# Layer norms in a four-layer transformer stack: the reciprocal root on GpSimd instead of ScalarE and VectorE

## The chip, the cores and the metric

The kernel runs on one core of a Trainium2 chip. A core has five engines with instruction queues of their own, each worked through in order: TensorE (PE in the profile; PEld is its weight load), VectorE (DVE), ScalarE (ACT), GpSimd (POOL) and SyncE (SP, which issues DMAs). The metric is the time of one execution on the device in microseconds (us); shown are three runs and one profiled execution.

## The reference

The input x has 4 x 256 tokens of 256 features, float32. Four layers follow each other, each with an attention to a small context and a feed-forward part, both gated and added to x:

```python
x = x + tanh(g_xattn[i]) * xattn_i(layernorm(x), ctx)
x = x + tanh(g_ffn[i]) * ffn_i(layernorm(x))

def _layernorm(x, axis=-1, eps=1e-05):
    m = jnp.mean(x, axis=axis, keepdims=True)
    v = jnp.var(x, axis=axis, keepdims=True)
    return (x - m) / jnp.sqrt(v + eps)
```

The layers differ. Layer 0: 16-head attention through a latent with rotary positions, and 16 experts of which 6 are used per token, beside a shared one. Layer 1: latent attention, and a feed-forward part with ternary weights and GELU. Layer 2: 16-head attention with a causal mask, and a single matrix with weights and tokens quantised to 8 bits. Layer 3: such attention, and 8 experts of which 2 are used, with a shared one. The output is x, 1024 x 256.

## The kernel before, in words

x stays in SBUF for the whole kernel, as 8 tiles of 128 tokens x 256 features. The tiles are worked on in two groups of four (512 tokens, `TPG` = 4 tiles to a group).

`layernorm(g, scalar, after)`, L425 to L453, normalises one group. VectorE computes the statistics of each tile (bn_stats L430, bn_aggr L433) into `mv`, 128 x 4 x 2. ScalarE takes the root of variance + eps for the four tiles at once, 128 x 4 (L435), and VectorE its reciprocal (L438), so that `rstd` holds a number for every token. Then each tile is shifted and scaled into `xn`: by VectorE in one instruction (L449), or, with `scalar=True`, by ScalarE (L446) from a `shift` that VectorE prepares (L442). `transposed` (L455 to L464) has PE transpose the four tiles (L461) into two PSUM buffers and copies them into `xT`; `evacuate` (L165 to L171) gives such copies by turns to ScalarE (L169) and to VectorE (L171). The projections (L476 and others) read `xT`.

The function is called 16 times, for two groups in each of the 8 half layers: in `attention0` (L722 for the first group and L805 for the second), `normalised` (L465, for the experts of layers 0 and 3), `attention1` (L950), `inputs1` (L1874, the feed-forward part of layer 1), at the end of that part for layer 2's first group (L1940), in the queries of layers 2 and 3 (L1045), and in `rounded` (L1998, the quantised part of layer 2). `rounded` and layer 3's queries pass `scalar=True`. At L805 two hints of order are passed as `after`: the first tile's statistics and the root are placed behind named instructions (`behind`, L141), without a semaphore.

ScalarE evaluates functions from tables that are loaded when the set changes (ACT_TABLE_LOAD rows). At the start a dummy activation on a 128 x 1 tile (`root`, L189 and L190) loads a table. The other functions are the exponential of the softmax (L484, and L1101 in layers 2 and 3), Tanh (L822, once), Silu (L1677, L1789 and in the experts) and Gelu (L1912).

Attention runs through `in_flight` (L519): for step i the scores and exponentials of token tile i are begun, `weights` (L486) normalises tile i-1 (VectorE sums L490 and reciprocal L491, then GpSimd multiplies 128 x 1024, L492), tile i-2 is transposed by PE (L506), copied by ScalarE (L507) and multiplied with the values (L714 in layers 0 and 1; L1109 and L1121 in layers 2 and 3), and tile i-3 is added to x (L517). The norms of the next half layer begin as soon as their four tiles of x are done, so the first group's norm often runs while the last tiles of attention are in flight.

GpSimd also does half of the rotary arithmetic, memsets, the indirect DMAs of the experts (L1386, L1485) and, in layer 2's quantised part, the additions to x (L2013, L2035). `ffn2` ends with matmuls that have no result (`kept_busy`, L510 to L514) while PE would otherwise have none.

The order of each engine's queue is made by the framework's scheduler from the data dependencies, priorities and hints such as those named; the kernel doesn't write it out. Tiles from pools (`xn`, `rstd`, `mv`) come round in a ring of buffers.

Of the kernel before, what the change touches and what calls it, by code (L numbers as in the profile page):

```python
# [30 lines left out]
F32 = mybir.dt.float32  # L31
# [4 lines left out]
AF = mybir.ActivationFunctionType  # L36
ALU = mybir.AluOpType
AX = mybir.AxisListType

P = 128  # L40
# [5 lines left out]
TPG = TH // P  # L46
# [4 lines left out]
EPS = 1e-5  # L51
# [46 lines left out]
def tile_flamingo(ctx: ExitStack, tc: tile.TileContext, a: dict, out: bass.AP):  # L98
    nc = tc.nc

    const = ctx.enter_context(tc.tile_pool(name="const", bufs=1))
# [36 lines left out]
    def small(shape, name, bufs=3, dtype=F32):  # L138
        return sb.tile(shape, dtype, tag=name, name=name, bufs=bufs)

    def behind(later, sooner):  # L141

        tc.add_manual_dep(
            later.ins,
            sooner.ins.name,
            mybir.DependencyInfo(mybir.DependencyClass.NoSync, mybir.DependencyReason.DATA),
            reason="not sooner",
        )
# [37 lines left out]
    nc.gpsimd.memset(ones, 1.0)  # L186
    eps = const.tile([P, 1], F32, tag="eps", name="eps")
    nc.gpsimd.memset(eps, EPS)
    root = small([P, 1], "root", 1)  # L189
    nc.scalar.activation(root, eps, AF.Sqrt)  # L190


    fixed = const.tile([P, FIXED], F32, tag="fixed", name="fixed")
# [231 lines left out]
    def layernorm(g, scalar=False, after=()):  # L425

        mv = small([P, TPG, 2], "mv")
        for i in range(TPG):
            st = small([P, 6], "st")
            made = nc.vector.bn_stats(st, x[g * TPG + i])  # L430
            if after:
                behind(made, after[0])
            nc.vector.bn_aggr(mv[:, i, :], st)  # L433
        rstd = small([P, TPG], "rstd")
        made = nc.scalar.activation(rstd, mv[:, :, 1], AF.Sqrt, bias=eps)  # L435
        if after:
            behind(made, after[1])
        nc.vector.reciprocal(rstd, rstd)  # L438
        xn = []
        if scalar:  # L440
            shift = small([P, TPG], "shift")
            nc.vector.scalar_tensor_tensor(shift, mv[:, :, 0], -1.0, rstd, ALU.mult, ALU.mult)  # L442
        for i in range(TPG):
            n = sb.tile([P, D], F32, tag="xn", name="xn", bufs=AHEAD + 2)
            if scalar:
                nc.scalar.activation(n, x[g * TPG + i], AF.Identity, bias=shift[:, i : i + 1], scale=rstd[:, i : i + 1])  # L446
                xn.append(n)
                continue
            kept["normal"] = nc.vector.tensor_scalar(  # L449
                n, x[g * TPG + i], mv[:, i, 0:1], rstd[:, i : i + 1], ALU.subtract, ALU.mult  # L450
            )
            xn.append(n)
        return xn  # L453
# [11 lines left out]
    def normalised():  # L465

        out = []
        for g in range(NG):
            xn = layernorm(g)
            out.append((transposed(xn), xn))  # L470
        return out
# [247 lines left out]
    def attention0(gate):  # L719


        xT = [transposed(layernorm(0))]  # L722
        fold_queries0(0)
        after = kept["copied"], kept["folded"]
# [77 lines left out]
        for n in range(6 * NQ + 2):  # L802
            f, m = divmod(n, 6)
            if n == 2:
                xT.append(transposed(layernorm(1, after=after)))  # L805
            if f < NQ:
                rotated(n)
                if m == 1 and f + 1 < NQ:
                    fold_queries0(f + 1)
                if m % 3 == 1 and f >= NQ - 2:  # L810
                    next(output)
            if wide is None:
                wide, rest = fold_scores0()
            if m == 3 and f < NQ:
                to_latent(f, 0)
            if m == 5:
                rest_to_latent(f)
            if m == 1 and f >= 1:
                to_latent(f - 1, 1)
            if n >= 6:  # L820
                next(later, None)
# [1374 lines left out]
```

## Time and profile before

| | |
|---|---|
| three runs | 826.5, 824.56, 826.2 us; median 826.2 |
| profiled execution | 824.72 us, of which 822.9 the span of the trace |
| mean granted clock of TensorE | 0.992 |
| busy PE / PEld | 776.0 us (94%) / 520.6 us (63%) |
| busy DVE / ACT / POOL | 497.2 us (60%) / 291.7 us (35%) / 246.0 us (30%) |
| ACT_TABLE_LOAD | 21, of 1.283 us each |
| roots (L435) | 16, 0.298 us each |
| reciprocals of them (L438) | 16, 0.170 us each |

The profile is that of one execution. A group line names the source line, engine and operation, then output<-inputs, shapes and the number of instructions; after the first bar stand busy us and the mean ns of one, after the second the idle time of the engine just before them and the instruction that ended most of it. A line of the timeline gives the start and length in us of a run of like instructions, and in square brackets the idle time of the engine ahead of it with what released it. A line of waits gives the waiting instruction, the one it waited for, and the us in total, the times and the longest. The granted clock is TensorE's, as a share of full speed.

### The profile page before, as it was taken

Reading aid. Unit: us, or ns where it says so; the run is one execution under the profiler, and the core shown is the slowest. Engines: PE = TensorE matmul, PEld = TensorE weight load, DVE = VectorE, ACT = ScalarE, POOL = GpSimd, SP = SyncE. Lnnn points to the kernel's source line nnn. Section 1 sums busy time; section 2 is a strip of 40 time slices with the busy share of each in tenths; the row PEclk is TensorE's granted clock in tenths of the full one; section 3 lists DMA queues with packets and bytes.
Section 4 is the critical chain, followed back from the end, with each engine's and each line's share of the span. In section 5 each row is a group of like instructions: output and inputs, shape, how many; then the busy total and the mean of one; then the engine's idle time right before and its main releaser. Section 6 shows DMA issues by size and latency. Waiting matters only on the chain. (4 is left out here: it accounts for less than half of the span.)

```text
span 822.9 us, 12507 instructions
## 1 busy us (share of the span) xinstructions
PE 776.0 (94%) x4507; PEld 520.6 (63%) x4510; DVE 497.2 (60%) x1146; ACT 291.7 (35%) x508; POOL 246.0 (30%) x211
## 2 busy tenths in 40 slices
PE   6999999898999999999999999998798899999994
PEld 5544433787564776766556566755445647999993
DVE  5565455874693455534878759888769564334331
ACT  3121112343421333422543568166455421233320
POOL 1355444322123344222021110024424103444332
PEclk9999999999999999999999999999999999999998
DMA  9510115800121253333930001630000102232211
GB/s 358 181 39 0 58 39 190 281 18 11 30 63 50 68 130 73 64 74 81 336 111 1 8 1 33 229 129 1 26 1 2 52 9 78 54 50 42 29 16 18
DMA packets 32467, 62.44 MB, mean 76 GB/s; under 512 B 5552, under 2 KB 19504, under 8 KB 31696
## 3 DMA queue, kind: packets, MB, share of 16 engines
q1 hardware_dynamic: 25008, 51.91, 18.3%
q0 software_dynamic: 7104, 9.41, 6.9%
q8 instruction: 39, 0.64, 0.3%
q10 hardware_dynamic: 288, 0.26, 0.1%
q14 instruction: 28, 0.23, 0.1%
HBM read 52.81 MB, written 9.27 MB: 75 GB/s over the span
## 5 line engine op out<-in xcount | busy, mean ns | idle before, releaser
L492 POOL TENSOR_TENSOR attn<-attn,sm 128x1024 f32<-128x1024 f32 x32 | 61.1, 1911 | 219.3 <-DVE sm L491 170.9
L476 PE MATMUL wide<-xT,big 128*128 128x512 f32 (+1 forms) x240 | 108.6, 600 | 1.1 <-DVE shared L1678 0.9
L742 DVE TENSOR_TENSOR rope<-wide,big 128x512 f32<-128x512 f32 x96 | 59.6, 684 | 51.9 <-PE wide L476 51.9
L476 PEld LDWEIGHTS wide<-xT,big 128*128 128x128 f32 (+1 forms) x240 | 43.4, 188 | 57.3 <-issue 49.3
L1451 PE MATMUL wide<-blk,still 128*128 128x128 f32 x640 | 74.8, 275 | 0.6 <-DVE blk L1423 0.6
L1451 PEld LDWEIGHTS wide<-blk,still 128*128 128x128 f32 x640 | 73.1, 192 | 0.8 <-issue 0.8
L714 PE MATMUL mm<-vo,attnT 128*128 128x256 f32 x256 | 58.6, 382 | 1.5 <-ACT attnT L507 1.5
L476 PE MATMUL wide<-xT,dense 128*128 128x512 f32 (+1 forms) x120 | 55.1, 598 | 0.0
L714 PEld LDWEIGHTS mm<-vo,attnT 128*128 128x128 f32 x256 | 47.8, 190 | 11.4 <-ACT attnT L507 3.3
L507 ACT COPY attnT<-mm 128x512 f32<-128x512 f32 x64 | 34.5, 587 | 43.3 <-PE mm L506 42.9
L490 DVE TENSOR_REDUCE sm<-attn 128x16 f32<-128x1024 f32 x32 | 38.7, 1209 | 15.2 <-ACT attn L484 13.8
L1413 DVE COPY still<-big 128x1024 f32 x20 | 13.9, 694 | 52.1 <-PE wide L1451 44.5
L1485 POOL DMA_INDIRECT out_dram<-ring,scratch x20 | 31.5, 1577 | 39.5 <-DVE ring L1478 15.6
L1485 POOL DMA_INDIRECT sums<-ring,big x17 | 26.8, 1575 | 48.5 <-ACT ring L1567 18.9
L1469 PE MATMUL mm<-big,hidden 128*128 x160 | 37.8, 380 | 1.4 <-DVE hidden L1462 1.4
L506 PE MATMUL mm<-ident,attn 128*128 128x128 f32 x256 | 34.6, 279 | 4.6 <-POOL attn L492 4.6
L1386 POOL DMA_INDIRECT xs<-xd,scratch x20 | 20.0, 1002 | 62.1 <-PE mm L1420 31.5
L506 PEld LDWEIGHTS mm<-ident,attn 128*128 128x128 f32 x256 | 29.9, 143 | 12.8 <-POOL attn L492 7.9
L1461 ACT ACTIVATE hidden<-wide 128x512 f32<-128x512 f32 x20 | 12.0, 598 | 71.2 <-PE wide L1451 65.7
L476 PEld LDWEIGHTS wide<-xT,dense 128*128 128x128 f32 (+1 forms) x120 | 21.5, 185 | 24.4 <-issue 22.7
L517 DVE SCALAR_TENSOR_TENSOR x<-mm,tg,x 128x256 f32<-128x256 f32 x44 | 20.4, 469 | 26.6 <-PE mm L714 15.0
L796 ACT COPY big<-mm 128x512 f32<-128x512 f32 x16 | 8.6, 589 | 67.9 <-PE mm L784 61.7
(363 smaller groups left out, 1575.8 us busy)
## 6 DMA issues: line engine op xcount, KB each, us to landing
big<-in_L_w_gate_up SPq DMA_DIRECT2D x8, 1024.0 KB, 12.0
big<-in_L_w_down SPq DMA_DIRECT2D x8, 512.0 KB, 9.0
w_L_qk<-in_L_qk SPq DMA_DIRECT2D x4, 896.0 KB, 7.3
big<-in_L_w SPq DMA_DIRECT2D x2, 1480.0 KB, 8.1
big<-in_L_w SPq DMA_DIRECT2D x2, 1110.0 KB
big<-in_L_wo SPq DMA_DIRECT2D x1, 2048.0 KB, 15.3
big<-in_L_w SPq DMA_DIRECT2D x2, 1024.0 KB, 5.3
xd<-xn SPq DMA_DIRECT2D x16, 128.0 KB, 1.9
```

Source lines behind the costliest of these rows:

```text
L476: nc.tensor.matmul(ps, w(c), xT[:, c, :], start=(c == 0), stop=(c == 1))
L490: nc.vector.tensor_reduce(sm, e, AX.X, ALU.add)
L492: nc.gpsimd.tensor_tensor(e, e, sm.unsqueeze(2).to_broadcast([P, groups, n]), ALU.mult)
L506: nc.tensor.transpose(ps[:, i * P : (i + 1) * P], ev[:, pr * P : (pr + 1) * P], ident)
L507: nc.scalar.copy(aT[:, half * 4 : half * 4 + 4, :].rearrange("p i t -> p (i t)"), ps)
L517: return nc.vector.scalar_tensor_tensor(x[t], ps, gate, x[t], ALU.mult, ALU.add)
L714: nc.tensor.matmul(ps[:, :D], aT[:, s, :], vo[:, s, :], start=(s == 0), stop=(s == NP - 1))
L742: nc.vector.tensor_tensor(m[:, s, :].rearrange("q (b t) -> q b t", t=S), ps[:, s, :].rearrange("q (b t) -> q b t", t=S), table, ALU.mult,)
L1386: nc.gpsimd.indirect_dma_start(out=xs, out_offset=None, in_=self.xd, in_offset=bass.IndirectOffsetOnAxis(ap=self.gather[:, b : b + 1].bitc ...
L1451: made = nc.tensor.matmul(ps[:, k, f : f + P], w[:, at : at + P], st[:, c * P : (c + 1) * P], start=(c == 0), stop=(c == 1),)
L1469: made = nc.tensor.matmul(ps[:, :D], hT[:, j * P : (j + 1) * P], self.w[:, bass.ds(r + j * D, D)], start=(j == 0), stop=(j == n - 1),)
L1485: nc.gpsimd.indirect_dma_start(out=self.sums[b % len(self.sums)], out_offset=bass.IndirectOffsetOnAxis(ap=self.scatter[:, b : b + 1].bitca ...
```

## The change

A constant tile `power`, 128 x 1, is set to -0.5 by GpSimd at the start. In `layernorm`, VectorE adds eps to the variance, and GpSimd raises the 128 x 4 result to the power of -0.5. ScalarE's root and VectorE's reciprocal are gone, so ScalarE no longer evaluates a root anywhere, and the dummy activation at the start loads the exponential's table. At L805 the second hint of order now applies to the power.

```diff
     eps = const.tile([P, 1], F32, tag="eps", name="eps")
     nc.gpsimd.memset(eps, EPS)
+    power = const.tile([P, 1], F32, tag="power", name="power")
+    nc.gpsimd.memset(power, -0.5)
     root = small([P, 1], "root", 1)
-    nc.scalar.activation(root, eps, AF.Sqrt)
+    nc.scalar.activation(root, eps, AF.Exp)
...
         rstd = small([P, TPG], "rstd")
-        made = nc.scalar.activation(rstd, mv[:, :, 1], AF.Sqrt, bias=eps)
+        nc.vector.tensor_scalar_add(rstd, mv[:, :, 1], EPS)
+        made = nc.gpsimd.tensor_tensor(rstd, rstd, power.to_broadcast([P, TPG]), ALU.pow)
         if after:
             behind(made, after[1])
-        nc.vector.reciprocal(rstd, rstd)
```

In the changed kernel's order of instructions ScalarE has 6 table loads: for the exponential at the start, Silu, the exponential, Gelu, the exponential and Silu.

## The prediction

> **What bounds the kernel now.** I read the page's busy times, then PE's waits, then the chain of waits around each of the 16 layer norms.
>
> ```profile
> PE 776.0 (94%) x4507; PEld 520.6 (63%) x4510; DVE 497.2 (60%) x1146; ACT 291.7 (35%) x508; POOL 246.0 (30%) x211
> ```
>
> PE works 776.0 of 822.9 us: 47 us are left, 6.5 of them before the first matmul. So an instruction taken from ScalarE, or given to GpSimd, counts only where PE waits. PE's waits (releaser after the arrow; us in all, times, longest):
>
> ```profile
> PE mm L461 <- DVE xn L449: 6.5, 1, 6.5
> ...
> PE mm L506 <- POOL attn L492: 4.6, 5, 1.7
> PE mm L1109 <- ACT attnT L507: 3.6, 9, 1.0
> ```
>
> Of the 16 norms only the first shows in "L461 <- xn". The others run while PE has attention or expert work, but their instructions stand in the queues between softmax steps. ScalarE's groups show what the roots cost there:
>
> ```profile
> L435 ACT ACT_TABLE_LOAD x8 | 10.3, 1283 | 0.1
> L484 ACT ACT_TABLE_LOAD x5 | 6.4, 1283 | 2.9 <-DVE attn L483 2.9
> ```
>
> Root and exponential need different function tables, so ScalarE loads one for 1.28 us at nearly every change. The chain itself, at the start:
>
> ```profile
> 5.04 0.30 DVE L433 BATCH_NORM_AGGREGATE mv<-st 128x2 f32<-128x6 f32 x2
> ...
> 5.37 0.30 ACT L435 ACTIVATE rstd<-mv,eps 128x4 f32<-128x4 f32 x1 [2.22 <-DVE mv L433]
> ...
> 5.70 0.18 DVE L438 RECIPROCAL rstd<-rstd 128x4 f32<-128x4 f32 x1 [0.25 <-ACT rstd L435]
> ...
> 5.92 1.38 DVE L449 TENSOR_SCALAR xn<-x,mv,rstd 128x256 f32<-128x256 f32 x4
> ```
>
> From the statistics (end 5.34) to the first normalised tile (5.92) is 0.58 us, two changes of engine among them.
>
> **What goes.** The order of the changed kernel has 6 table loads in place of 21, and no roots: ScalarE is relieved of 15 x 1.283 + 16 x 0.298 = 24.0 us. (The tanh's load goes too.) VectorE loses 16 reciprocals (0.17 each) and gets 16 small adds; the nearest row, 128x2 at L1962, is 0.169 us: nothing changes there.
>
> **What comes.** GpSimd computes 16 powers of 128x4. The trace has no power. Below: GpSimd's products are 294 ns for 128x64 and 404 for 128x128, so 1.72 ns an element on top of 184 ns: a power as cheap as a product takes 0.19 us. Above, the longest ordinary elementwise operation, L492 with 128x1024:
>
> ```profile
> L492 POOL TENSOR_TENSOR attn<-attn,sm 128x1024 f32<-128x1024 f32 x32 | 61.1, 1911 | 219.3 <-DVE sm L491 170.9
> ```
>
> A power is a routine (logarithm, product, exponential) rather than one step. The nearest rows of routines on GpSimd are its indirect DMAs, 1.00 us (L1386) and 1.58 (L1485). I take X = 1.0 us, with ends 0.19 and 1.9. With the add (0.17) and the 0.03 to 0.06 us that one change of engine takes in the rows, statistics to first tile becomes X + 0.25; so a norm for which PE waits costs X - 0.33.
>
> VectorE runs in order, and its first tile (L449) follows right behind the add: in the 12 norms that normalise there it stands still for X; and the power waits behind whatever GpSimd has queued.
>
> **Norm by norm** (time of before; X = 1.0):
> - First, 5.4: PE waits. +0.7. (Loading the exponential's table at the start in place of the root's, at 1.66, changes nothing; x lands at 3.49.)
> - Second (13.5), and those at 457, 519, 532.6, 643.6: PE has 4 us and more of queued work: 0. Gone is the load at 540.03, behind it a gap of 0.13: -0.1.
> - 181, inside attention 0: the power is queued behind the product L492 that ends at 181.28, VectorE stands until about 182.3, and its copy of vo (L171, 182.02) and row maximum (L482) come later; PE's queue covers part. A gap of 0.99 at 193.95 shrinks, as the load at 185.37 is gone. X - 0.4 = +0.6.
> - 206.7: PE reaches the second group's transposes about X late; 0.3 come back from gaps of 0.91 and 0.41 up to 221. +0.7.
> - 391 and 399 (layer 1): gaps of 0.66 (406.83) and 0.30 (421.66) stand behind exp loads that go: -1.0.
> - 485.6: 0.24 at 486.68 goes: -0.2.
> - 572.1, layer 2's quantised input. Here the load does harm. ScalarE and PE:
>
> ```profile
> 570.86 1.28 ACT L435 ACT_TABLE_LOAD   x1
> 572.15 0.30 ACT L435 ACTIVATE rstd<-mv,eps 128x4 f32<-128x4 f32 x1
> 572.36 1.05 ACT L507 COPY attnT<-mm 128x512 f32<-128x512 f32 x2
> ```
>
> ```profile
> 572.98 0.91 PE L1109 MATMUL mm<-attnT,values 128*32 128x128 f32 x16 [1.03 <-ACT attnT L507]
> 574.38 1.76 PE L1121 MATMUL mm<-w_L,ctxTok 128*128 128x256 f32 x4 [0.49 <-ACT ctxTok L1118]
> 575.94 1.91 PE L506 MATMUL mm<-ident,attn 128*128 128x128 f32 x8
> ```
>
>  The copy waits for load and root, and PE for the copy 1.03; other tiles' wait is 0.29: -0.74. After it the granted clock is 0.84 and 0.73 in the two 4 us windows, and three groups take 1.76, 1.91 and 0.58 us against 1.13, 1.04 and 0.43 before: 1.65 us. I give it 6 in 10 to go with the gap: -1.0.
> - 586.3: PE waits for xn (L2024 <- L2009), power for root: X - 0.5 = +0.5.
> - 598.5 and 601.5, layer 3's inputs, the dearest place:
>
> ```profile
> 597.30 2.77 POOL L2035 TENSOR_TENSOR x<-x,y 128x256 f32<-128x256 f32 x4 [3.95 <-DVE y L2034]
> ```
>
>  The powers come behind all four additions, so the first starts at 600.07 where the root started at 598.45. VectorE's shift waits for it, and behind the shift stand the second group's statistics (1.4 us) and add, then the second power. On ScalarE, in the new order, the second group's first tile stands ahead of the copy of the first group's xT. Counted on: 600.07 + X + 0.2 (shift) + 1.4 + 0.2 + X + 0.2 + 0.5 (tile) + 0.6 (copy) = 605.2; before, PE started L476 at 602.67: 2.6 (0.6 + 2X). The clock is 0.67 in 596 to 600 already; a longer gap may hold it down by what it held at 572 (1.7, again 6 in 10): +1.0.
> - 652.6 (second group of the last FFN): PE's transposes wait with nothing ahead of them in the new order: X + 0.2 = +1.2.
>
> Sum: 0.7 - 0.1 + 0.6 + 0.7 - 1.0 - 0.2 - 0.74 - 1.0 + 0.5 + 2.6 + 1.0 + 1.2 = +4.3 us. It moves 7 us for each us of X (terms 1, 181, 206, 586, 652 once, layer 3 twice). At X = 0.19: -1.4; at 1.9: +10.6, to which up to 2 come where covers of 4 us run out. Profiled execution 824.7 + 4.3 = 829.0. The median of the runs, 826.2, is 1.5 above the profiled one: 830.5.
>
> **A rule against the row.** The Trainium skill, "ScalarE: Activation LUTs", section "What ACT_TABLE_LOAD costs", states about 1283 ns for the load and as much again for a drain of the pipeline. The load agrees to the nanosecond; the drain does not show, since at 570.86 the load begins where the exponential ends and the root follows 1.29 later. By the page's 2.66 us each, 15 switches would be 40 us of ScalarE, by the rows 19; PE waits for three or four either way.
>
> The 128x4 shift at 573 took 1.80 us beside a product L492 of GpSimd, against 0.14 at 599.30. The skill's "GPSIMD Engine Reference", sections "Specifications" and "Engine selection", speaks against the change: VectorE is named for elementwise work, and GpSimd shares its memory interfaces with VectorE instructions that have two SBUF inputs. The shift has two and agrees. If the new adds met such products, the sum would be up to 1.6 more at each of the norms at 181, 572 and 652; by the page they are spared, having one input. It gives no price for a power.
>
> **Rivals.**
> 1. The power is cheap, X of 0.2 to 0.4: for it, 512 elements are few, and a small product would be 0.19; against it, a power isn't one step. Then the freed loads win, above all that at 570.86 with its clock dip whole (-0.7 more) and no lasting dip in layer 3 (-1.0): -1.4 - 1.7 = -3.1, 823.1. It decides below X of 0.45. This is the other side: faster.
> 2. The power is worked out element by element: 512 elements in X of about 5 us. Against it: GpSimd's products show 1.72 ns per element of a partition. Then 4.3 + 4 x 7 = 32, and the norms at 13, 457, 519, 532 and 643 lose their cover, 3 each: 47; 877.
> 3. Layer 3's queue doesn't bind: the schedule's order there is no loss because PE's later work fills it (layer 3 has waits on ScalarE anyway). The 3.6 go: 826.9, no change. Against it: PE has nothing but L476 to go to.
>
> **How the numbers follow.** A measurement of this kernel can tell about 0.3%, 2.5 us, from no change. The sum with X between 0.45 and 2.5: 0.50, of which 0.08 stays within 2.5 us (X below 0.75) and 0.42 is slower. Rival 1: 0.24 (0.16 faster, 0.08 the same). Rival 2: 0.16, slower. Rival 3: 0.10, the same. Together faster 0.16, the same 0.26, slower 0.58. Range: rival 1 at its best with a us to spare, 822, up to X = 2.5 (4.3 + 1.5 x 7 = 14.8) and some 5 us of lost cover, 846; outside it lie rival 2 and a little.
>
> **What would show it.** Right: a row of GpSimd's power near 1 us; ScalarE's busy time down by 24; no wait over 0.4 at 573; a new PE wait of 2 to 3 us for xT ahead of L476 near 600, and one of about 1 us for xn at 652. Wrong: a power under 0.4 or over 2.5 us, which shifts all direct waits by the same; a clock in 572 to 580 still under 0.9 with the gap gone; a wait of VectorE on GpSimd at 181 that PE's queue covers, so that the softmax in flight loses nothing.

## The result and the profile after

The changed kernel took 835.7 us (median of four, 833.62 to 838.03) against 826.35: a ratio of 1.0111, interval 1.0092 to 1.0131. A second series of six gave 837.41 and 1.0118 (1.0097 to 1.0140). The forecast of 830.5 had the direction and less than half of the size. The profiled execution took 838.03 us, its span is 836.3 against 822.9: 13.4 us more. It is the slowest of its four, as the profiled ones of again, apart and wide_first below are of theirs, while that of before is among its fastest, so the two profiles stand 4 us further apart than the medians. Its line numbers are 2 above those of before from L188 on.

The page of the changed kernel:

```profile
PE 785.1 (94%) x4507; PEld 524.6 (63%) x4510; DVE 496.3 (59%) x1146; ACT 268.4 (32%) x477; POOL 262.6 (31%) x228
```

PE's idle time rose from 46.9 to 51.2 us, by 4.3. But PE's busy time, for the same 4507 instructions, rose from 776.0 to 785.1. The loss is one third waiting and two thirds slower work. ScalarE lost 23.3 us of work; the time got back about 2 of them, at 572 (below). The power, in GpSimd's groups:

```profile
L438 POOL TENSOR_TENSOR rstd<-rstd,power 128x4 f32<-128x4 f32 x16 | 16.2, 1014 | 94.3 <-DVE rstd L437 89.6 <-DVE ident L393 4.3
```

1.01 us each, against the estimate of 1.0. That was luck: the estimate was the length of an indirect DMA, and no run shows how GpSimd works out a power, only how long it takes. PE's waits:

```profile
PE mm L463 <- DVE xn L451: 8.6, 3, 7.4
...
PE mm L508 <- POOL attn L494: 3.5, 4, 1.7
PE mm L1111 <- ACT attnT L509: 3.3, 10, 0.5
PE mm L2026 <- DVE xn L2011: 2.2, 2, 1.8
PE mm L463 <- ACT xn L448: 2.0, 1, 2.0
...
PE mm L508 <- DVE vo L171: 1.4, 1, 1.4
...
PE mm L478 <- ACT xT L169: 1.1, 1, 1.1
```

Three norms now hold PE through xn (before: one), layer 3 holds it by 2.0 and 1.1, and the longest wait for attnT fell from 1.0 to 0.5: the gap at 573 is gone. At the start (GpSimd, then VectorE):

```profile
5.86 1.04 POOL L438 TENSOR_TENSOR rstd<-rstd,power 128x4 f32<-128x4 f32 x1 [4.35 <-DVE ident L393]
```
```profile
6.94 1.38 DVE L451 TENSOR_SCALAR xn<-x,mv,rstd 128x256 f32<-128x256 f32 x4 [1.11 <-POOL rstd L438]
```

Statistics to first tile: 1.44 us (5.50 to 6.94) in place of 0.58.

Where 13.3 us of the profiled executions' difference arose, by the shift of each PE instruction, its start less that of its twin of before (medians over 10 us):

| place (us of before) | forecast | shift gained |
|---|---|---|
| start | +0.7 | +1.33 |
| 181, attention 0 | +0.6 | +0.43 |
| 207 to 260, experts of layer 0 | +0.7 | +4.25 |
| 270 to 421, with layer 1 | -1.0 | -0.23 |
| 457 | 0 | +1.69 |
| 486 to 533 | -0.3 | -0.21 |
| 572, quantised input | -1.7 | -2.10 |
| 586 | +0.5 | +0.56 |
| 598 to 615, layer 3 | +3.6 | +4.01 |
| 652 to 680, experts of layer 3 | +1.2 | +3.59 |

Two places hold most of the miss, both where an expert layer begins. PE at the first, before and after:

```profile
205.06 3.70 PE L476 MATMUL wide<-xT,big 128*128 128x512 f32 x8 [0.24 <-ACT xT L169]
208.59 1.04 PE L461 MATMUL mm<-ident,xn 128*128 128x128 f32 x8
209.47 1.86 PE L1153 MATMUL mm<-fixed,xT 128*128 128x16 f32 x16
211.17 1.96 PE L476 MATMUL wide<-xT,big 128*128 128x512 f32 x4
212.97 1.85 PE L1153 MATMUL mm<-fixed,xT 128*128 128x16 f32 x16
214.68 5.40 PE L476 MATMUL wide<-xT,big 128*128 128x512 f32 x12
220.98 1.98 PE L476 MATMUL wide<-xT,big 128*128 128x512 f32 x4 [0.91 <-DVE shared L1678]
```

```profile
209.56 1.32 PE L463 MATMUL mm<-ident,xn 128*128 128x128 f32 x8 [0.76 <-DVE xn L451]
210.71 1.86 PE L1155 MATMUL mm<-fixed,xT 128*128 128x16 f32 x16
212.41 1.10 PE L478 MATMUL wide<-xT,big 128*128 128x512 f32 x2
213.36 2.32 PE L1155 MATMUL mm<-fixed,xT 128*128 128x16 f32 x16
215.51 10.89 PE L478 MATMUL wide<-xT,big 128*128 128x512 f32 x18
...
258.50 3.70 PE L478 MATMUL wide<-xT,dense 128*128 128x512 f32 x8 [1.43 <-DVE h L1575]
```

The wait for xn is 0.76, of the 1.0 counted. But the 18 wide passes (L478) then take 0.60 us each, where 8 took 3.70, 0.46 each, before. The windows of the changed kernel (stretch, its length, then busy us and instructions of PE, PEld, DVE, ACT, POOL, and the granted clock):

```profile
211.16:214.57 3.41, 3.41 (x27) 2.94 (x26) 0.44 (x1) 0.23 (x1) 0.00 (x0) 1.00 0.25 82
214.57:217.98 3.41, 3.41 (x9) 2.10 (x9) 1.22 (x5) 0.64 (x2) 0.58 (x2) 0.50 0.00 0
217.98:221.40 3.41, 3.41 (x5) 1.35 (x4) 3.27 (x24) 1.64 (x2) 1.80 (x3) 0.50 0.00 0
```

The same window of before:

```profile
214.57:217.98 3.41, 3.41 (x11) 1.57 (x11) 2.07 (x5) 2.28 (x3) 1.43 (x3) 1.00 0.00 0
```

The clock is 0.50 for 6.8 us. In the 3.41 us just ahead of it PE is busy throughout, so no gap in them explains it; but 26 weight loads fill 2.94 of them: 24 belong to the router's products (L1155), each of which loads 128 columns to move 16.

The 6.8 us at half clock are 3.4 us of lost work (estimate, half of them). The waits of this stretch come to 0.7 more than before: 0.76 for xn and 1.43 at 258.5 are new, and gaps of 0.91, 0.41 and 0.17 are gone. In layer 3 the new wait for xn is 0.48 and before's gap of 0.51 at 663.95 is gone, so of the +3.59 there the 6.8 us at half clock are nearly all. PE there, one row of before and then the changed kernel:

```profile
663.95 3.70 PE L476 MATMUL wide<-xT,w_L_sgu 128*128 128x512 f32 x8 [0.51 <-DVE shared L1790]
```

```profile
664.14 1.32 PE L463 MATMUL mm<-ident,xn 128*128 128x128 f32 x8 [0.48 <-DVE xn L451]
665.29 1.85 PE L1155 MATMUL mm<-fixed,xT 128*128 128x8 f32 x16
667.00 1.10 PE L478 MATMUL wide<-xT,w_L_sgu 128*128 128x512 f32 x2
667.94 2.87 PE L1155 MATMUL mm<-fixed,xT 128*128 128x8 f32 x16
670.66 10.30 PE L478 MATMUL wide<-xT,w_L_sgu 128*128 128x512 f32 x18
```

The granted clock of this execution is 0.50 in five stretches ahead of the tail: 214.6 (6.8 us), 463.7 (3.4), 600.3 (3.4), 610.5 (3.4) and 668.5 (6.8). Before has two, 574.7 and 595.2, of 3.4. Their starts within one execution lie whole multiples of 3.413 us apart: there is a grid, of windows of 3.413 us.

### The profile page after: what moved, and what is told of

Same layout as the page of the kernel before. It is cut to its first block, busy times and chain, and to the rows that moved or that the text cites. A ratio compares the mean times of both kernels' runs of the same rounds, so it can differ in the third digit from the quotient of the medians.

```text
span 836.3 us, 12485 instructions
## 1 busy us (share of the span) xinstructions
PE 785.1 (94%) x4507; PEld 524.6 (63%) x4510; DVE 496.3 (59%) x1146; ACT 268.4 (32%) x477; POOL 262.6 (31%) x228
## 5 line engine op out<-in xcount | busy, mean ns | idle before, releaser
L478 PE MATMUL wide<-xT,big 128*128 128x512 f32 (+1 forms) x240 | 111.4, 613 | 0.2 <-ACT xT L169 0.2
L494 POOL TENSOR_TENSOR attn<-attn,sm 128x1024 f32<-128x1024 f32 x32 | 61.1, 1911 | 151.0 <-DVE sm L493 110.7
L478 PEld LDWEIGHTS wide<-xT,big 128*128 128x128 f32 (+1 forms) x240 | 44.6, 193 | 57.4 <-issue 50.6
L478 PE MATMUL wide<-xT,dense 128*128 128x512 f32 (+1 forms) x120 | 55.5, 599 | 1.9 <-DVE h L1575 1.4
L438 POOL TENSOR_TENSOR rstd<-rstd,power 128x4 f32<-128x4 f32 x16 | 16.2, 1014 | 94.3 <-DVE rstd L437 89.6
L478 PEld LDWEIGHTS wide<-xT,dense 128*128 128x128 f32 (+1 forms) x120 | 21.4, 185 | 26.2 <-issue 21.3
L508 PEld LDWEIGHTS mm<-ident,attn 128*128 128x128 f32 x256 | 29.3, 142 | 13.4 <-POOL attn L494 6.3
```

Source lines behind the costliest of these rows:

```text
L478: nc.tensor.matmul(ps, w(c), xT[:, c, :], start=(c == 0), stop=(c == 1))
L494: nc.gpsimd.tensor_tensor(e, e, sm.unsqueeze(2).to_broadcast([P, groups, n]), ALU.mult)
L508: nc.tensor.transpose(ps[:, i * P : (i + 1) * P], ev[:, pr * P : (pr + 1) * P], ident)
```

## The experiments

**Theory A**: the clock is set for a stretch of the grid by how much of the array the stretch before it used; the new waits and the new order of PE's products (all transposes of the second group, then the router's narrow products of both groups almost together) bring two places below the line. **Rival B**: the waits alone do it. **Rival C**: such stretches come and go in any kernel, and the profile was an unlucky one.

**again**: the changed kernel, no edit.

> The changed kernel once more, with more runs, beside the others on one chip. The first profile of it has half-clock stretches at 214.6 (6.8 us), 463.7 (3.4), 600.3 (3.4), 610.5 (3.4) and 668.5 (6.8), all beginning on one grid of 3.413 us; before has two of 3.4 us. Theory A (the changed order of PE's products sets the two long ones: the router's narrow products of both token groups stand almost together): both or one of the long stretches in most executions, clock 0.979 to 0.988, 833 to 838 us. Rival B (PE's waits for the power at 209 and 664 set them): the same here. Rival C (such stretches come and go in any kernel and the first profile was an unlucky one): a median nearer to 831, with a clock near 0.99.

837.41 us (832.58 to 838.26), five of six executions at a mean clock of 0.981, one (832.58) at 0.987; before on this chip 0.989 to 0.993. The profile has the same five stretches within 0.3 us, and the other executions at 0.981 have as much half clock, so C falls for the two long ones.

**apart**: the second group's router products later.

```diff
             g, i = divmod(t, TPG)
+            if t == TPG:
+                yield
             for c in range(2):
...
             unit(*of)
+            if i == 0:
+                continue
+            if i == 1:
+                next(steps)
```

> The changed kernel, but the router's products of the second group are issued after the second unit of the shared expert, so that 12 wide passes (L476 of before) stand between the two groups' narrow ones in place of 2, in layers 0 and 3. Powers and waits stay. Theory A: the stretches of half clock near 214 and 668 go, mean clock 0.988 or more, 829 to 831 us (835.7 less 4 to 7). Rival B: both stretches stay, 835. Rival C: no change of the median beyond a us.

833.46 (829.46 to 837.29), ratio 1.0073 (1.0050 to 1.0096), above the 829 to 831 that A expected. In the profile the stretch at 668 is gone; that at 213 stayed, behind the wait of 0.8 and 16 narrow products, and there are others at 155.1 and 602.2. And the later router made the routing late:

```profile
242.53 0.87 PE L1324 MATMUL mm<-big 128*128 128x43 f16 x8 [2.23 <-DVE big L1322]
```

with a new stretch of half clock from 243.8. Moving work away from a low window made another.

**together**: before, with the narrow products held together and no power.

```diff
-                mm2(ps[:n, k, :], lambda c: s13[:, k, c, at : at + n], xT[g])
+                mm2(ps[:n, k, :], lambda c: s13[:, k, c, at : at + n], xT[g],
+                    kept["router"] if (g, f, k) == (0, 1, 0) else None)
```

(mm2 puts its matmuls `behind` that product; the same in layer 3.)

> The kernel before, with root and reciprocal, but with the router's products of both groups held together (no wide passes between them) in layers 0 and 3 by hints of order; no power anywhere. Theory A: new stretches of half clock near 213 and 656, each 3.4 or 6.8 us long and costing 1.7 to 3.4 us; 829 to 832 us in place of 826.3. Rival B: no such stretches, 826 to 827. Rival C: the same as B on average.

830.21 (828.22 to 832.40), ratio 1.0047 (1.0031 to 1.0063). PE and windows in layer 0:

```profile
211.31 3.84 PE L1155 MATMUL mm<-fixed,xT 128*128 128x16 f32 x32
215.00 7.52 PE L476 MATMUL wide<-xT,big 128*128 128x512 f32 x13
```
```profile
211.88:215.29 3.41, 3.39 (x29) 3.28 (x29) 1.18 (x3) 2.54 (x4) 0.00 (x0) 1.00 0.02 4
215.29:218.70 3.41, 3.41 (x5) 1.35 (x4) 2.33 (x9) 1.59 (x2) 1.82 (x3) 0.50 0.00 0
```

No wait and no power, a PE that is busy for 3.39 of 3.41 us, and the clock halves right behind the narrow products. So B alone can't explain it: no wait is needed. In layer 3 this execution had no stretch there, against the expectation. Its grid can be the reason: with the use of the array counted as in the last section, a window that begins from 659.3 to 661.9 would have a use under 0.40, 2.6 of the 3.4 us that the grid can choose from; those of this execution begin at 659.0 and 662.4.

**gmult**: a product by 1.0 for the power, in the changed kernel's order; the normalisation is left out.

```diff
-        nc.vector.tensor_scalar_add(rstd, mv[:, :, 1], EPS)
-        made = nc.gpsimd.tensor_tensor(rstd, rstd, power.to_broadcast([P, TPG]), ALU.pow)
+        nc.vector.tensor_scalar(rstd, mv[:, :, 1], EPS, 0.2, ALU.add, ALU.min)
+        made = nc.gpsimd.tensor_tensor(rstd, rstd, power.to_broadcast([P, TPG]), ALU.mult)
```

> The changed kernel with a product by 1.0 in place of the power (VectorE's add also takes a minimum with 0.2, so that the rows are scaled by about 0.2 and not by 1/sqrt(variance + eps): the normalisation is left out). The order of all engines is that of the changed kernel. The product should take 0.19 us in place of 1.01. The terms that count the power's time (one each at the start, 181, 206, 586, 652, two in layer 3) give 7 x 0.82 = 5.7 us less. Theory A: the long stretches at 214 and 668 stay, since the order of the narrow products stays: about 835.7 - 5.7 = 830, clock under 0.988. Rival B: the stretches go too, 823 to 824.

The total, 855.04, says nothing: without normalisation tokens go to other experts: PE has 126 instructions more than in again, and layer 3's experts take some 30 us longer. Up to 810 us the instructions are the same, and there PE stands 10.1 us ahead of the changed kernel, 3.2 behind before.

```profile
L438 POOL TENSOR_TENSOR rstd<-rstd,power 128x4 f32<-128x4 f32 x16 | 3.2, 200 | 98.0 <-DVE rstd L437 86.0 <-PE mm L927 6.7 <-DVE ident L393 4.9
```

A product takes 0.20 us, near the lower end of 0.19. Against the expectation under A, no long stretch stands at 211 or 660: with the same order, but without the wait, the clock held. That doesn't yet show that the wait is needed, since this is one execution and its grid may have missed the place. Counted in the same way, a window that begins from 209.6 to 210.7 or from 657.4 to 659.0 would have a use under 0.40; those of this execution begin at 208.4 and 659.0, with 0.47 and about 0.40. What holds with together is that the narrow products can be enough; how much the wait adds to them is argued, not shown.

**wide_first**: power and all; the shared expert's whole first unit (8 wide passes in place of 4) ahead of the second group's transposes.

```diff
+            xns.append(layernorm(g))
+            last = beside() if g else None
+            xT.append(transposed(xns[g], after=last))
```

(`beside` is `up(0, 0)`; the transposes are put `behind` its last matmul.)

> The changed kernel, power and all, but in layers 0 and 3 the shared expert's whole first unit (8 wide passes in place of 4) is issued ahead of the second group's transposes, by a hint of order: in layer 0 this is PE's order of before. So PE works where it waited 0.76 us for xn at 209 and 0.48 at 664, and the router's narrow products stand less close. Theory A, as the four runs have changed it (the clock is halved after a window of 3.413 us in which the array was used under about 0.4 of its rows and columns; wait and narrow products together bring it there): no long stretches near 214 and 668, 3.4 + 2.6 us less there and the two waits gone (1.2 us), 829 to 832 us and a clock of 0.985 or more. Rival (the stretches follow from the power itself, whatever PE does): 837 as before, clock 0.981.

829.67 (826.56 to 832.03), ratio 1.0025 (1.0008 to 1.0041): 7.7 us under the changed kernel (again), with all 16 powers in place. PE in layer 0:

```profile
207.28 3.70 PE L481 MATMUL wide<-xT,big 128*128 128x512 f32 x8 [0.24 <-ACT xT L169]
210.81 1.04 PE L463 MATMUL mm<-ident,xn 128*128 128x128 f32 x8
211.69 1.86 PE L1159 MATMUL mm<-fixed,xT 128*128 128x16 f32 x16
213.39 1.96 PE L481 MATMUL wide<-xT,big 128*128 128x512 f32 x4
215.19 1.85 PE L1159 MATMUL mm<-fixed,xT 128*128 128x16 f32 x16
216.90 5.40 PE L481 MATMUL wide<-xT,big 128*128 128x512 f32 x12
```

This is the order of before; the wait is filled with work that has to be done anyway, and the stretches at 214 and 668 are gone, the rise of the shift at both places too. The grid is not the reason here: wherever a window is laid over 203 to 222 or 655 to 672, its use comes out at 0.53 or more. So the loss at the two places follows PE's order, not the power as such, which settles the main cause. Which of the two things that this order does counts more, filling the wait or spreading the narrow products, it doesn't tell. The profile has other stretches, at 154.1, 270.2, 461.3, 597.8 (6.8 us) and 608.1.

**filled**: 8 and 4 filling matmuls for 6 and 2.

```diff
-            kept_busy((6, 2)[g], ps_wide()[:, 0], last)
+            kept_busy((8, 4)[g], ps_wide()[:, 0], last)
```

> The changed kernel with 8 and 4 filling matmuls in place of 6 and 2 in layer 2's quantised part (they have no result), so that PE is busy where it waited 1.8 us at 599 and 2.0 at 607. Everything else as in the changed kernel. Theory A: the half-clock stretches at 600.3 and 610.5 go (1.7 us each where PE worked), the waits stay as filled time: 837.4 less 2 to 3.4, about 834.5, stretches at 214, 463 and 668 as before. Rival (the clock does not depend on what PE does in a wait): 837 to 838, and the fillers' extra 0.2 us.

835.16 (832.86 to 839.47), ratio 1.0100 (1.0070 to 1.0129). The stretch at 600 is gone; that at 610 stayed, for the wait moved: PE did its fillings and the transposes and then waited 2.91 for xT. Near the expected size, but by itself too scattered to decide.

**gtwice**: a second power ahead of each.

```diff
+        nc.gpsimd.tensor_tensor(rstd, rstd, unit.to_broadcast([P, TPG]), ALU.pow)
```

> The changed kernel with a second power ahead of each (exponent 1.0, so the result is the same): 2.03 us in place of 1.01 on GpSimd, 16 times. The prediction's slope of 7 us per us of the power's time gives 7.1 more in waits of PE; with covers of 4 us that run out at the other norms up to 2 more. Without further change of the clock: 837.4 + 7 to 9, 844 to 847. If the waits set the clock as theory A has it, one to three more half-clock stretches come, up to 850. A rival in which the direct waits are hidden and the clock alone is the loss: under 840.

851.85 (849.92 to 853.90), ratio 1.0304 (1.0278 to 1.0329): 14.4 more than again for some 1.0 us of power, and above the 850 that was the most expected. PE's idle time grew by 9.6 (51.2 to 60.8), near the 7 to 9 foreseen; the other part is busy time at half clock, 785.1 to 789.0, and the spread of executions.

**hybrid**: the power for layer 2's quantised input alone.

```diff
+        if power_of:
+            nc.vector.tensor_scalar_add(rstd, mv[:, :, 1], EPS)
+            made = nc.gpsimd.tensor_tensor(rstd, rstd, power.to_broadcast([P, TPG]), ALU.pow)
+        else:
+            made = nc.scalar.activation(rstd, mv[:, :, 1], AF.Sqrt, bias=eps)
...
-        xn = layernorm(g, True)
+        xn = layernorm(g, True, power_of=True)
```

> The power for layer 2's quantised input alone (the norms at 572 and 586), root and reciprocal in the 14 others. The table load at 570.86 that held up the copies goes, with the half-clock stretch behind it: the changed kernel gained 2.1 us there, and lost 0.5 at 586. Expected 826.3 - 1.6 = 824.7, clock 0.993 or more; if the load only moves (to the next root, at 598, where ScalarE waits for VectorE anyway), the same. Rival: the stretch comes by the grid's phase and not by that gap: 826 as before.

828.38 (824.49 to 831.00), ratio 1.0013 (0.9997 to 1.0029), and not the 824.7 expected. PE gains its 2.1 us between 560 and 585, and the stretch at 574 is gone; but this execution has others, at 154.0, 594.3 (6.8 us), 604.6 and 662.6. The last one stands in layer 3's experts, where this kernel has root and reciprocal: in before too, a window that begins from 654.9 to 656.0 would have a use under 0.40. So layer 3's place is near the line without the change, and how much of its +3.59 is the change's own a single profile doesn't tell. The three executions at a clock of 0.994 took 824.5 to 825.9.

**wide_l3root**: as wide_first, with the root in layer 3.

```diff
-            xn = layernorm(g, layer == 3)
+            xn = layernorm(g, layer == 3, power_of=layer != 3)
```

> As wide_first (power, shared expert's first unit ahead of the second group's transposes), but layer 3's two norms take root and reciprocal again. The prediction's dearest term, 2.6 us of waits and 1.0 of the clock around 600, should go, since the root does not stand behind GpSimd's additions: 829.7 less 2.6 to 3.6, 826 to 827, in the trace the shift against before stays flat across 590 to 615 in place of rising by 3.8. One table load comes back (root) and one exponential load, both where ScalarE waits. Rival (the queue behind the additions is no loss in itself, the clock is all of it): no more than 1 us less, 829.

828.23 (826.42 to 831.12), ratio 1.0021 (1.0006 to 1.0036): by the medians 1.4 less than wide_first, by the ratios 0.3, not 2.6 to 3.6. In the profiles the shift across 590 to 615 rises by 1.6 us in place of 3.7. The undoing wasn't clean, since the scheduler put the second root ahead of the first group's tiles on ScalarE:

```profile
602.84 0.30 ACT L441 ACTIVATE rstd<-mv,eps 128x4 f32<-128x4 f32 x1 [2.04 <-DVE mv L435]
603.16 2.57 ACT L453 ACTIVATE xn<-x,shift,rstd 128x256 f32<-128x256 f32 x5
```

so PE still waited 1.77 us there. This run gives no clean price of layer 3's term.

**best**, **before_busy** and **both**: these are hybrid, before and the changed kernel in turn, each with the unit of wide_first ahead and more filling.

```diff
-            kept_busy((6, 2)[g], ps_wide()[:, 0], last)
+            kept_busy((8, 3)[g], ps_wide()[:, 0], last)
```

(8 and 4 in both.)

> The power for layer 2's quantised input alone, the shared expert's first unit ahead of the second group's transposes, and 8 and 3 filling matmuls in place of 6 and 2. Each of these took something away in the runs so far: the gap at 573, the narrow products' company in layer 3's experts (660), and the waits around 592 to 602. If the windows of low use are what costs, 823 to 825 with fewer runs above 826 than the version with the power there alone (824.5 to 831.0). Rival (the spread is chance that no filling changes): 828 again.

> The control for the version before this in the list: the same order and fillings, root and reciprocal everywhere, no power. If the power at 572 is worth its 1.6 us, this is 1 to 2 us above that version, 825 to 826.5. If the order and the fillings are all of it, the same time as that version.

> The changed kernel, all 16 powers, with both helps for the clock: the shared expert's first unit ahead of the second group's transposes (829.7 alone) and 8 and 4 filling matmuls in layer 2's quantised part. If windows of low use are what made the loss larger than the waits that were counted, the stretches at 600 and 610 go as well, 1.7 to 3.4 us less than with the order alone: 826.5 to 828.5, clock 0.990 or more. What is left over before is then the counted waits less the gain at 572. Rival (fillings do not help, as the first trial of them left open): 829.7.

best: 826.06 (825.09 to 829.58), ratio 1.0001 (0.9987 to 1.0015). before_busy: 826.55 (824.40 to 828.64), ratio 1.0000 (0.9986 to 1.0015). The expected 823 to 825 did not come, and the power at 572 is worth 0.5 us by the medians and nothing by the ratios; no version measured better than before. both: 828.67, ratio 1.0027 (1.0016 to 1.0039), and its twelve executions lie within 828.08 to 829.46, at clocks of 0.992 to 0.994; a stretch at 603.9 is left, so the filling did not take all of them away, and the time is just above the 826.5 to 828.5 expected. With all 16 powers, keeping the array in use took 8.7 us off the changed kernel (7.5 by the ratios) and with them its spread; 2.4 are left, for the waits of the start, of 181 and of layer 3, less the gain at 572.

## Why the prediction was too low

Right: the power's length (1.01 for 1.0), by luck, and the waits that follow from it. Attention 0 (+0.4 for +0.6), the quantised input (-2.1 for -1.7, clock stretch included), 586, layer 3 (+4.0 for +3.6) came as counted. In layer 3 the queue was the one named:

```profile
603.07 2.78 POOL L2037 TENSOR_TENSOR x<-x,y 128x256 f32<-128x256 f32 x4 [4.01 <-DVE y L2036]
605.80 1.02 POOL L438 TENSOR_TENSOR rstd<-rstd,power 128x4 f32<-128x4 f32 x1
608.31 1.01 POOL L438 TENSOR_TENSOR rstd<-rstd,power 128x4 f32<-128x4 f32 x1 [1.49 <-DVE rstd L437]
```
```profile
607.71 1.91 PE L463 MATMUL mm<-ident,xn 128*128 128x128 f32 x8 [2.02 <-ACT xn L448]
610.67 5.30 PE L478 MATMUL mm<-xT,w_L 128*128 128x512 f32 x8 [1.05 <-ACT xT L169]
```

The power begins as the four additions end, PE waits 2.0 and 1.05 (the longer one for xn, not for xT), and the next passes run at half clock (0.66 us each): all three terms. The waits are 2.5 more than before's 0.57, as the prediction's own count gives (605.2 less 602.67 is 2.5, where it wrote 2.6). But their split, 0.6 + 2X, was wrong. In gmult, with a product of 0.20:

```profile
600.36 2.16 PE L463 MATMUL mm<-ident,xn 128*128 128x128 f32 x8 [1.90 <-ACT xn L448]
602.99 6.05 PE L478 MATMUL mm<-xT,w_L 128*128 128x512 f32 x8 [0.46 <-ACT xT L169]
```

That is still 1.8 more than before, not 1.0, with half clock behind it: most of the loss in layer 3 is the place behind the additions, and less of it the power's length.

The step that failed is "206.7: PE reaches the second group's transposes about X late ... +0.7", and with it "652.6 ... +1.2". The waits for xn were 0.76 and 0.48, less than forecast, and the waits of the two stretches together came to +0.7 (the forecast figure, but with a wait of 1.43 in it that nobody had counted) and to nothing; what was left out is the clock behind them, about 3.4 us at each place. The prediction asked for the clock only at 572 and 600, where before already had a low row, and took for granted that elsewhere a wait costs its own length. Behind these two waits stand the router's narrow products, closer together in the new order, which the prediction had read for the queues and not for the clock: +4.25 and +3.59 in place of +0.7 and +1.2, 5.9 of the 9.0 us by which the profiled execution exceeds the sum of 4.3. wide_first takes both away without touching the power.

The rest: 457 (+1.7 for 0) is another such stretch, but not the change's alone: together and before_busy, without any power, have it at 461 and 458. The gains in layer 1 (-1.0) were a misreading: the gap of 0.66 ahead of L690 is still there in the changed kernel (L692, 0.66), with no table load near it; only 0.15 came. At the start the power costs 0.86; the remaining 0.5 is not the power's, since the shift at 10 us lies between +0.15 and +1.65 in the kernels with it and between -0.1 and +1.9 in those without.

Of VectorE's 16 adds 13 took the 0.15 to 0.17 us foreseen; three that met a product of GpSimd (L494) took 0.62, 1.07 and 1.57. The first:

```profile
182.00 0.62 DVE L437 TENSOR_SCALAR rstd<-mv 128x4 f32<-128x4 f32 x1
```

It ends with the product (182.59), and so do the other two. That this instruction would be spared was a wrong use of the Trainium skill's "GPSIMD Engine Reference", section "Specifications", which names VectorE's two-port mode as well as two inputs. In which mode the adds ran no run here shows.

Of the prediction's rivals none came. What stays open: why single executions of one kernel differ by up to 8 us (apart). It goes with the mean clock, and the place of the grid decides which windows fall low, as the counts under together and gmult show; but that the grid's place is what differs from one execution to the next was not measured by itself.

## What to carry to other kernels

Price a new wait of TensorE twice: by its length, and by what the clock does behind it when narrow, weight-bound matmuls stand near. A full busy column is no proof of a clock that holds; count columns moved, and look at the order in which they stand in the built program, not at the queues alone. Fill a wait with wide work that is due anyway: in wide_first that took back 7.7 of the 11 us.

## What the runs showed of the hardware

**The clock follows the array's use in fixed windows.** I counted each pass with its moved columns times 0.9 ns (32-bit: a 512-column pass of L476 takes 0.46 us) or 0.58 (16-bit: L1065, 0.295), weighted by the share of the array's 128 rows and 128 columns it occupies (passes whose width the trace does not give count as 256 columns, by their length), in windows of the grid of 3.413 us, over the 14 profiles of this case, the first 20 us and the end left out. Of the windows at full clock:

| use of the array (estimate) | windows | next one at half clock |
|---|---|---|
| under 0.35 | 29 | 29 |
| 0.35 to 0.45 | 27 | 18 |
| over 0.45 | 3137 | 0 |

PE's busy share draws no such line: in the 47 windows ahead of a half clock it goes from 0.06 to 1.00. Nor do the moved columns without the weight of rows and columns: by them these windows reach 1.25, and most of the others lie below that. The bounds were not tried on another kernel. The stretch at 463.7 fits: its window ends in 64*64 products (L692), which fill a quarter of the array, and a wait of 1.5.

The Trainium skill's "TensorE: Matmul & The Clock Gate", "Part 1: The HAM clock gate", gives a free-running window of 3413 ns and half rate after an idle window. The length and the grid agree with the traces here; the condition does not: in together PE was busy for 3.39 of 3.41 us ahead of the half clock. The measurement decides: low use is enough.

**A power on GpSimd** of 128x4 takes 1.01 us, a product of the same shape 0.20.
